# Cross-attention on one core: first Wq chunk in three transfers, second x block on two queues, and a new written order

## The chip, the cores and the metric

The kernel runs on one core of one Trainium2 chip. The metric is the device time of one execution in microseconds; smaller is better. The times shown are medians over runs of the same program.

## The reference, cut to what matters

The input x has 2 batches of 2048 tokens with 640 channels; the context has 2 batches of 154 tokens with 1024 channels, the first 77 of them text, the other 77 of a second kind ("ip"). There are 20 heads of 32 channels. All is fp32.

```python
q = split_heads(x @ Wq.T, 20)
k, v       = split_heads(text @ Wk.T),    split_heads(text @ Wv.T)
k_ip, v_ip = split_heads(ip @ Wk_ip.T),   split_heads(ip @ Wv_ip.T)
attend = lambda q, k, v: softmax(q @ k.T / sqrt(32)) @ v
out = merge_heads(attend(q, k, v)) + merge_heads(attend(q, k_ip, v_ip))
return out @ Wo.T + bo + x
```

## The kernel before, in words

The matrices reach the kernel transposed, so that the contracted dimension lies on the 128 partitions. The 640 channels are 5 chunks of 128, four heads to a chunk. The tokens of a batch are four blocks of 512, two to a half-batch. A **unit** u is one chunk of one half-batch: u = 0 to 19, in pairs; the pair 2q, 2q+1 is the attention number q (chunk q mod 5 of batch q div 5).

The work of a unit, by the words of the written order:

- `q.u.h`: five 128x512 matmuls on PE (TensorE, L195) make the queries of block h; `cq.u.h` copies and scales them on ACT (ScalarE, L205).
- `R0.u`, `R1.u`, `R2.u`: scores of the unit's three groups of token tiles (L233), each into four PSUM banks. A group has 3 tiles (24 PE records a group, since an fp32 product counts twice), in odd units 3, 2 and 2. The ninth tile of an even unit's third group belongs to the next unit, so `R2.0` needs `cq.1.0` for its last tile.
- `K` copies the four banks to SBUF on ACT (L245), `M` takes row maxima on DVE (VectorE, L258), `S` subtracts them (L272; on POOL, the GpSimd engine, or with the suffix `.d` on DVE), `E` is the exponential on ACT (L279), `D` and `I` sum and invert on DVE (L304, L311), `N` multiplies (L316, POOL), `T` transposes on DVE (L323).
- `A.q`: attention (L332) for both units of q, after all six `T`; `CA.q` copies the result on ACT.

Around it stand the key and value products `k.c.t`, `v.c.t` (L134, eight 128x154 matmuls, 16 PE records, one for each chunk c and kind t of context) with their copies `ck`, `cv`, and a detour of the values: `SQ` transposes them on DVE (L144), `VW` writes them to DRAM, `VS` reads them back spread over partitions. The output projection of batch 0 uses seven products in place of eight on sums of blocks (`W`, `G` on POOL or DVE at L404 and L434, products `m` at L493 and L503, `o` at L474, sums `cm`, `co`), that of batch 1 another scheme of 33 products (`F` at L857, weight and token sums `V` at L835 and L837 and `X` at L843, output sums `Y` at L803 and L805). Loads are words too: `LK` a key or value weight, `LQ` a Wq chunk, `LX` a block of x of batch 1.

Every engine works its instructions strictly in the order in which they are written, and that order is one long list of words, `SCHEDULE`, worked off by `emit`. The word after `@` names the PSUM banks, `.d` or `.p` the engine of a sum. The list sets what PE meets when, and which of DVE and POOL does a subtraction or a small sum. In front of it the opening is written out by hand:

```python
queues = nc.sync, nc.scalar
for k in range(NC):
    load_x(queues[k % 2])
    queues[1 - k % 2].dma_start(out=wqs[0][:, k, :], in_=WqT[ts(k, P), :P])
for _ in range(NC):
    load_x()
```

A transfer is issued by SP (SyncE, `nc.sync`) or by ACT (`nc.scalar`). Eight semaphores serve them in turn, so the issue of each transfer waits until the one eight places before it has landed; what stands behind it on its queue waits too. Names in the orders below: bank_79 to bank_86 are the banks 0 to 7, x_92 to x_95 the four blocks of x, wq_87 and wq_88 the two places for Wq chunks, aT the place of the key and value weights.

Of the kernel before, what the change touches and what calls it, by code (L numbers as in the profile page):

```python
# [9 lines left out]
F32 = mybir.dt.float32  # L10
# [10 lines left out]
def kernel(  # L21
# [25 lines left out]
    nc = tc.nc  # L47
# [5 lines left out]
    NH = 2  # L53
# [471 lines left out]
    slices.extend((i, k) for i in range(NHB) for k in range(NC))  # L525
    queues = nc.sync, nc.scalar
    for k in range(NC):
        load_x(queues[k % 2])
        queues[1 - k % 2].dma_start(out=wqs[0][:, k, :], in_=WqT[ts(k, P), :P])
    for _ in range(NC):  # L530
        load_x()
    load_wq(1)
    half = NCC // 2
    for k in (0, half):
        nc.sync.dma_start(  # L535
            out=wo_ct[:, ds(k * B * LT, half * B * LT)].rearrange("p (k n) -> p k n", k=half),
            in_=ctxT[ds(k * P, half * P), :].rearrange("(k p) n -> p k n", p=P),
        )
        load_w(k // half)
    for _ in range(NH * NC):  # L540
        load_x()
    load_w(2)
    load_w(3)
    nc.sync.dma_start(out=bo_sb, in_=bo.rearrange("(c p) -> p c", p=P))
# [5 lines left out]
    FIRST = ((0, 0), (0, 1), (2, 0))  # L550
    for n, (u, h) in enumerate(FIRST):
        queries(u, h, banks[G + n])
        take_queries(u, h, banks[G + n])
    for t in range(2):

        ps = halves[t][G - 2 + t]
        project_kv(t, ps)
        for b in range(B):
            nc.scalar.copy(kT[:, 0, b, t, :], keys_in(ps)[:, b])  # L559
# [82 lines left out]
    def emit(word):  # L642
# [27 lines left out]
        elif k == "fe":  # L670
            fetch(x, PARTS[y])
        elif k == "LO":
            load_wo()
        elif k == "LF":
            for part in PARTS:
                fetch(0, part)
# [223 lines left out]
```

## Time and profile before

| | |
|---|---|
| median of 3 runs | 498.87 us (498.44 to 499.19) |
| profiled execution | 499.62 us |
| its span, first to last instruction | 497.8 us |
| TensorE clock granted | 1.00 |
| PE, DVE, POOL, ACT busy | 98%, 89%, 80%, 49% of the span |
| moved by DMA | 70.15 MB, mean 141 GB/s |

How its lines are read. In the timeline a row is: start in us, length, engine, line, operation, output tile <- input tiles, shapes, count; in brackets the idle time just before it and what ended that. PEld is the weight load of PE, SPq and ACTq are the DMA issues of SP and ACT. A wait row is: engine and line that waited <- engine or transfer waited for, us in total, times, longest. A row of the chain (the work that ended last, followed back) is: start, length, engine, tile, line, count. A group row is: line, engine, operation, names, shapes, count | busy us, mean ns | idle us before and its releasers. A row by stretches of time is: from:to, length, then the busy us of PE, PEld, DVE, ACT and POOL, the granted clock, the DMA share and GB/s.

### The profile page before, as it was taken

Reading aid. Unit: us, or ns where it says so; the run is one execution under the profiler, and the core shown is the slowest. Engines: PE = TensorE matmul, PEld = TensorE weight load, DVE = VectorE, ACT = ScalarE, POOL = GpSimd, SP = SyncE. Lnnn points to the kernel's source line nnn. Section 1 sums busy time; section 2 is a strip of 40 time slices with the busy share of each in tenths; the row PEclk is TensorE's granted clock in tenths of the full one; section 3 lists DMA queues with packets and bytes.
Section 4 is the critical chain, followed back from the end, with each engine's and each line's share of the span. In section 5 each row is a group of like instructions: output and inputs, shape, how many; then the busy total and the mean of one; then the engine's idle time right before and its main releaser. Section 6 shows DMA issues by size and latency. Waiting matters only on the chain.

```text
span 497.8 us, 9753 instructions
## 1 busy us (share of the span) xinstructions
PE 489.1 (98%) x4114; PEld 287.1 (58%) x4114; DVE 440.8 (89%) x407; ACT 241.7 (49%) x423; POOL 398.4 (80%) x170
## 2 busy tenths in 40 slices
PE   8999999999999999999999999999999999999997
PEld 4658545667449555556656677565555565444442
DVE  0078999999997999999995999999999999997995
ACT  1157666667646677658526734325687561100000
POOL 0009997999959999999967799996998999349691
PEclk9999999999999999999999999999999999999999
DMA  8972640241915628826047525671375012410026
GB/s 276 353 201 68 163 112 1 66 103 49 260 42 183 178 77 269 310 80 224 18 144 260 170 84 162 213 255 47 121 255 182 18 35 77 156 67 19 0 95 243
DMA packets 66988, 70.15 MB, mean 141 GB/s; under 512 B 3712, under 2 KB 46720, under 8 KB 66944
## 3 DMA queue, kind: packets, MB, share of 16 engines
q1 hardware_dynamic: 66224, 68.81, 43.8%
q8 instruction: 32, 0.52, 0.4%
q10 hardware_dynamic: 720, 0.72, 0.4%
q14 instruction: 12, 0.10, 0.1%
HBM read 58.21 MB, written 11.30 MB: 140 GB/s over the span
## 4 chain that ended last, share of the span: by engine, by line
PE 88%; DMA 4%; DVE 4%; SPq 2%; ACT 1%; issue 1%; ACTq 0%
PE bank L195 32%; PE bank L857 11%; PE bank L332 11%; PE bank L233 10%; PE bank L493 9%; PE bank L134 8%; PE bank L474 4%; PE bank L503 2%; DMA x<-in_x_dram 2%; DVE pb L323 2%; DMA aT<-in_L_xattn_Wv_dram 2%; SPq L167 1%; DVE den L304 1%; SPq L535 1%; SPq L124 0%
## 5 line engine op out<-in xcount | busy, mean ns | idle before, releaser
L272 POOL TENSOR_TENSOR pb<-pb,mx 128x1848 f32<-128x1848 f32 (+1 forms) x54 | 160.2, 2980 | 52.8 <-DVE mx L258 52.7
L316 POOL TENSOR_TENSOR pb<-pb,rden 128x1848 f32<-128x1848 f32 (+1 forms) x59 | 172.2, 2935 | 14.8 <-ACT aT L355 5.9
L195 PE MATMUL bank<-x,wq 128*128 128x512 f32 x400 | 179.9, 599 | 0.9 <-DMA x<-in_x_dram 0.8
L258 DVE TENSOR_REDUCE mx<-pb 128x24 f32<-128x1848 f32 (+1 forms) x60 | 109.4, 1842 | 34.6 <-ACT pb L245 34.5
L195 PEld LDWEIGHTS bank<-x,wq 128*128 128x128 f32 x400 | 73.7, 190 | 85.9 <-issue 81.0
L245 ACT COPY pb<-bank 128x462 f32<-128x462 f32 (+1 forms) x240 | 102.2, 533 | 40.3 <-PE bank L233 37.9
L279 ACT ACTIVATE pb<-pb 128x1848 f32<-128x1848 f32 (+1 forms) x60 | 94.3, 1590 | 51.3 <-POOL pb L272 49.5
L323 DVE STREAM_TRANSPOSE pb<-pb 128x1920 f32<-128x1920 f32 (+1 forms) x60 | 114.1, 1922 | 2.1 <-POOL pb L316 1.8
L304 DVE TENSOR_REDUCE den<-pb 128x24 f32<-128x1848 f32 (+1 forms) x60 | 109.8, 1836 | 1.2 <-ACT pb L279 0.8
L233 PEld LDWEIGHTS bank<-kT,qT 32*128 32x128 f32 x1280 | 44.8, 184 | 24.9 <-issue 17.9
L233 PE MATMUL bank<-kT,qT 32*128 32x154 f32 x1280 | 55.9, 305 | 0.6 <-ACT kT L559 0.3
L332 PE MATMUL bank<-pb,v 32*32 32x512 f32 x1600 | 55.3, 597 | 0.7 <-DVE pb L323 0.6
L134 PEld LDWEIGHTS bank<-wo_ct,aT 128*128 128x128 f32 x320 | 43.2, 188 | 7.3 <-issue 3.5
L134 PE MATMUL bank<-wo_ct,aT 128*128 128x154 f32 x320 | 45.7, 296 | 1.4 <-DMA aT<-in_L_xattn_Wv_dram 1.0
L205 ACT ACTIVATE qT<-bank 128x512 f32<-128x512 f32 x40 | 23.9, 602 | 46.1 <-PE bank L195 46.1
L332 PEld LDWEIGHTS bank<-pb,v 32*32 32x32 f32 x1600 | 29.5, 103 | 23.0 <-issue 11.3
L474 PE MATMUL bank<-aT,wo_ct 128*128 128x512 f32 x80 | 36.3, 595 | 0.0
L493 PE MATMUL bank<-aT,wo_ct 128*128 128x256 f32 x128 | 32.8, 389 | 0.1
L493 PEld LDWEIGHTS bank<-aT,wo_ct 128*128 128x128 f32 x128 | 23.3, 190 | 7.0 <-issue 3.9
L805 DVE TENSOR_TENSOR x<-x,bank 128x512 f32<-128x512 f32 x36 | 23.3, 682 | 3.6 <-PE bank L857 3.5
L474 PEld LDWEIGHTS bank<-aT,wo_ct 128*128 128x128 f32 x80 | 15.0, 190 | 16.4 <-issue 15.6
L857 PE MATMUL bank<-pb 128*128 128x512 f32 x48 | 22.7, 594 | 0.0
(74 smaller groups left out, 351.1 us busy)
## 6 DMA issues: line engine op xcount, KB each, us to landing
x<-in_x_dram SPq DMA_DIRECT2D x20, 1280.0 KB, 7.2
out_dram<-acc SPq DMA_DIRECT2D x20, 256.0 KB, 2.5
x<-in_x_dram SPq DMA_DIRECT2D x18, 256.0 KB, 5.4
acc<-in_x_dram SPq DMA_DIRECT2D x16, 256.0 KB, 3.9
out_dram<-x SPq DMA_DIRECT2D x15, 256.0 KB, 2.1
v<-scr SPq DMA_DIRECT2D x40, 80.0 KB, 3.5
wq<-in_L_xattn_Wq_dram SPq DMA_DIRECT2D x9, 320.0 KB, 4.5
aT<-in_L_xattn_Wk_dram SPq DMA_DIRECT2D x5, 512.0 KB, 5.5
```

The source lines that it names most:

```text
L134: nc.tensor.matmul(keys_in(out), loaded[n][:, k, :], cT[:, k, :, t, :], start=(k == 0), stop=(k == NCC - 1))
L195: nc.tensor.matmul(pq, wqs[q % 2][:, k, :], xs[place_of(u, h)][:, k, :], start=(k == 0), stop=(k == NC - 1),)
L233: nc.tensor.matmul(ps[g][:, ts(t, 2 * L)], qTs[(v, h)][g * D : (g + 1) * D, ts(st, P)], kT[g * D : (g + 1) * D, c, b].rearrange("p t l -> ...
L245: nc.scalar.copy(keys_of(u, s)[:, :, g], ps[g][:, : n * 2 * L].rearrange("p (n l) -> p n l", n=n))
L258: nc.vector.tensor_reduce(mx, rows_of(u, s), AX.X, ALU.max, negate=by_rows(u, s))
L272: eng.tensor_tensor(rows_of(u, s), rows_of(u, s), maxs[(u, s)].unsqueeze(3).to_broadcast([P, n, 2, L]), ALU.subtract)
L279: nc.scalar.activation(e, e, AF.Exp)
L304: nc.vector.tensor_reduce(dens[(u, s)], rows_of(u, s), AX.X, ALU.add)
L316: eng.tensor_tensor(rows_of(u, s), rows_of(u, s), rdens[(u, s)].unsqueeze(3).to_broadcast([P, n, 2, L]), ALU.mult)
L323: nc.vector.transpose(p, p)
L332: nc.tensor.matmul(pa[r][g * D : (g + 1) * D, :], v4[rows, g, k, :], zones[rows, :, g, k, :], start=(k == 0), stop=(k == NK - 1),)
L493: nc.tensor.matmul(part, w_of[m][:, kp, op], t_of(m, b, i)[:, kp], start=(op == kp == 0 and m in (1, 2, 5)), stop=(op == 1 and kp == 1 and ...
```

## The change

Three edits.

1. The first Wq chunk goes in three transfers (128, 256 and 256 rows) in place of five, and the five slices of the second x block alternate between ACT's and SP's queue in place of SP alone.
2. What stood written out between these loads and the list (the loads of the second Wq chunk, the context, the first four key and value weights, the third and fourth x block and the bias; the first three query products; the first two key products) becomes words at the head of the list: `LQ.1 LC.0 LK.0 ...`. PE's order up to the second key product is the same as before; the copies of the first keys stay two for each product.
3. The list is another one. Its words are the same beside the new head; their order, the banks, and the engine of some sums differ. Up to `A.9`, the subtractions S1.0, S0.10, S1.15, S1.17 and the sums G5.0, G4.0, G5.1 go from DVE to POOL, and S0.1, S1.10, S1.13 from POOL to DVE. Behind it 22 of the `V` sums stood on DVE before and 15 do now; of the `X` sums ten did and ten do, not all the same.

The diff, with the list cut to its first lines:

```diff
-    slices.extend((i, k) for i in range(NHB) for k in range(NC))
+    slices.extend((i, k) for i in range(NH) for k in range(NC))
     queues = nc.sync, nc.scalar
+    WQ_PARTS = (0, 1), (1, 3), (3, NC)
     for k in range(NC):
         load_x(queues[k % 2])
-        queues[1 - k % 2].dma_start(out=wqs[0][:, k, :], in_=WqT[ts(k, P), :P])
-    for _ in range(NC):
-        load_x()
-    load_wq(1)
-    half = NCC // 2
-    for k in (0, half):
+        if k < len(WQ_PARTS):
+            ks = slice(*WQ_PARTS[k])
+            queues[1 - k % 2].dma_start(
+                out=wqs[0][:, ks, :],
+                in_=WqT[ks.start * P : ks.stop * P, :P].rearrange("(k p) o -> p k o", p=P),
+            )
+    for k in range(NC):
+        load_x(queues[1 - k % 2])
+
+    def load_context(n):
+        half = NCC // 2
...
-        load_w(k // half)
-    for _ in range(NH * NC):
-        load_x()
-    load_w(2)
-    load_w(3)
-    nc.sync.dma_start(out=bo_sb, in_=bo.rearrange("(c p) -> p c", p=P))
...
-    FIRST = ((0, 0), (0, 1), (2, 0))
-    for n, (u, h) in enumerate(FIRST):
-        queries(u, h, banks[G + n])
-        take_queries(u, h, banks[G + n])
-    for t in range(2):
-
-        ps = halves[t][G - 2 + t]
-        project_kv(t, ps)
-        for b in range(B):
-            nc.scalar.copy(kT[:, 0, b, t, :], keys_in(ps)[:, b])
...
-        "R0.0@5476 LK.5 K0.0 M0.0 S0.0.d R1.0@2103 K1.0 M1.0 S1.0.d q.1.0@5 cq.1.0 v.0.0@3 cv.0.0 R2.0@5047 K2.0 "
...
+        "LQ.1 LC.0 LK.0 LC.1 LK.1 lx.2.0 lx.2.1 lx.2.2 lx.2.3 lx.2.4 lx.3.0 lx.3.1 lx.3.2 lx.3.3 lx.3.4 LK.2 LK.3 LB q.0.0@4 cq.0.0 q.0.1@5 cq.0.1 q.2.0@6 cq.2.0 k.0.0@2 ck.0.0 k.0.1@7 ck.0.1 "
+        "R0.0@6754 K0.0 R1.0@1320 K1.0 q.1.0@6 cq.1.0 M0.0 S0.0.d R2.0@5407 M1.0 S1.0 K2.0 M2.0 S2.0 R0.1@2316 "
...
+        elif k == "LC":
+            load_context(x)
+        elif k == "LB":
+            nc.sync.dma_start(out=bo_sb, in_=bo.rearrange("(c p) -> p c", p=P))
+        elif k == "lx":
+            nc.sync.dma_start(out=xs[x][:, y], in_=xT[ts(y, P), ts(x, TB)])
```

More of the change, by code (lines that the diff above doesn't have):

```diff
@@ L522, in take_product @@
             nc.vector.tensor_tensor(t, t, ps.rearrange("p (op t) -> p op t", op=2), ALU.add)
-    slices.extend((i, k) for i in range(NHB) for k in range(NC))
+    slices.extend((i, k) for i in range(NH) for k in range(NC))
     queues = nc.sync, nc.scalar
+    WQ_PARTS = (0, 1), (1, 3), (3, NC)
     for k in range(NC):
         load_x(queues[k % 2])
-        queues[1 - k % 2].dma_start(out=wqs[0][:, k, :], in_=WqT[ts(k, P), :P])
-    for _ in range(NC):
-        load_x()
-    load_wq(1)
-    half = NCC // 2
-    for k in (0, half):
+        if k < len(WQ_PARTS):
[8 more added lines that the diff above has]
+        half = NCC // 2
         nc.sync.dma_start(
-            out=wo_ct[:, ds(k * B * LT, half * B * LT)].rearrange("p (k n) -> p k n", k=half),
-            in_=ctxT[ds(k * P, half * P), :].rearrange("(k p) n -> p k n", p=P),
-        )
-        load_w(k // half)
-    for _ in range(NH * NC):
-        load_x()
-    load_w(2)
-    load_w(3)
-    nc.sync.dma_start(out=bo_sb, in_=bo.rearrange("(c p) -> p c", p=P))
+            out=wo_ct[:, ds(n * half * B * LT, half * B * LT)].rearrange("p (k n) -> p k n", k=half),
+            in_=ctxT[ds(n * half * P, half * P), :].rearrange("(k p) n -> p k n", p=P),
+        )
     warm = pb[:, 0].rearrange("p g l -> p (g l)")[:, :P]
@@ L696, in emit @@
         elif k == "ck":
-            nc.scalar.copy(kT[:, x, :, y, :], keys_in(at[name[1:]]))
+            if x:
+                nc.scalar.copy(kT[:, x, :, y, :], keys_in(at[name[1:]]))
+            else:
+                for n in range(B):
+                    nc.scalar.copy(kT[:, x, n, y, :], keys_in(at[name[1:]])[:, n])
         elif k == "cv":
```

136 rows, old and new, of the table SCHEDULE are left out of this document.

## The prediction

> **What bounds the kernel now.** I read the page's busy times first, then the waits of PE, the chain that ended last, the opening in order of time, and the idle time of DVE and POOL.
>
> ```profile
> PE 489.1 (98%) x4114; PEld 287.1 (58%) x4114; DVE 440.8 (89%) x407; ACT 241.7 (49%) x423; POOL 398.4 (80%) x170
> ```
>
> PE (TensorE) works 489.1 of 497.8 us. Neither order adds or drops a matmul, so what can change is PE's idle time and the cost of passing from one kind of matmul to another. The waits of PE (total, times, longest, in us):
>
> ```profile
> PE bank L134 <- DMA aT<-in_L_xattn_Wv_dram: 1.0, 1, 1.0
> PE bank L195 <- DMA x<-in_x_dram: 0.8, 1, 0.8
> PE bank L332 <- DVE pb L323: 0.6, 1, 0.6
> PE bank L134 <- ACT pb L245: 0.5, 1, 0.5
> PE bank L857 <- ACT aT L360: 0.3, 1, 0.3
> PE bank L233 <- ACT kT L559: 0.3, 1, 0.3
> PE bank L233 <- ACT pb L245: 0.3, 1, 0.3
> ```
>
> Beside the start of the program these seven rows are all its idle time: 3.8 us, and that is about the whole prize. But PE is not alone. The waits of DVE and POOL:
>
> ```profile
> DVE mx L258 <- ACT pb L245: 34.5, 11, 25.3
> POOL pb L272 <- DVE mx L258: 52.7, 12, 36.7
> ```
>
> DVE's longest wait is the opening (25.3 us); after it DVE waits for copies only 9 us in all until the last attention. It is nearly as full as PE, and attention A.q can't start before the last transpose T of its two half-batches. How close that is, at A.1 and A.9 (timeline and chain, transpose first, then PE):
>
> ```profile
> 110.64 1.51 DVE L323 STREAM_TRANSPOSE pb<-pb 128x1280 f32<-128x1280 f32 x1 [0.52 <-POOL pb L316]
> 112.44 5.45 PE bank L332 x150
> 426.19 1.50 DVE L323 STREAM_TRANSPOSE pb<-pb 128x1280 f32<-128x1280 f32 x1
> 427.74 5.52 PE L332 MATMUL bank<-pb,v 32*32 32x512 f32 x160 [0.61 <-DVE pb L323]
> ```
>
> T2.3 ends at 112.15 and A.1 follows 0.3 us later; T2.19 ends at 427.69 and A.9 follows at once, having waited 0.6. So PE's time is worth something only where DVE keeps up.
>
> **The opening.** The same bytes in the same order of need, but 8 transfers instead of 10 for the first block and its weights. Each transfer waits at issue for the one eight places before it. Timeline and DMA rate (last column GB/s):
>
> ```profile
> 4.13 4.21 SPq L167 DMA_DIRECT2D x<-in_x_dram  x6
> 4.32 0.34 ACTq L529 DMA_DIRECT2D wq<-in_L_xattn_Wq_dram  x1
> 4.35 2.90 PE L195 MATMUL bank<-x,wq 128*128 128x512 f32 x6
> 8.04 10.57 PE L195 MATMUL bank<-x,wq 128*128 128x512 f32 x24 [0.80 <-DMA x<-in_x_dram]
> 3.50:4.00 0.50, 0.50 (x5) 0.50 (x3) 0.00 (x0) 0.00 (x0) 0.00 (x0) 1.00 1.06 388
> 6.50:7.00 0.50, 0.50 (x2) 0.00 (x0) 0.00 (x0) 0.00 (x0) 0.00 (x0) 1.00 1.00 208
> 7.00:7.50 0.50, 0.24 (x1) 0.00 (x0) 0.00 (x0) 0.00 (x0) 0.00 (x0) 1.00 0.69 240
> 10.06 0.60 ACT L205 ACTIVATE qT<-bank 128x512 f32<-128x512 f32 x1 [4.09 <-PE bank L195]
> ```
>
> The ninth and tenth (last x slice, last Wq part) go out only at 4.13 and 4.32, and two us later the rate dips. What SP issues at the start, before and after (x_92 is the first block of x, x_93 the second, wq_87 and wq_88 the Wq chunks):
>
> ```order
> L167 DMA x_92<-in_x_dram 128x512
> L529 DMA wq_87<-in_L_xattn_Wq_dram 128x128
> L167 DMA x_92<-in_x_dram 128x512
> L529 DMA wq_87<-in_L_xattn_Wq_dram 128x128
> L167 DMA x_92<-in_x_dram 128x512 [waits DMAHW1_49]
> L167 DMA x_93<-in_x_dram 128x512 [waits DMAHW2_49]
> ```
>
> ```order
> L167 DMA x_92<-in_x_dram 128x512
> L532 DMA wq_87<-in_L_xattn_Wq_dram 128x2x128
> L167 DMA x_92<-in_x_dram 128x512 x2
> L167 DMA x_93<-in_x_dram 128x512 [waits DMAHW1_49]
> L167 DMA x_93<-in_x_dram 128x512 [waits DMAHW3_49]
> L186 DMA wq_88<-in_L_xattn_Wq_dram 128x5x128 [waits DMAHW5_49]
> ```
>
> Everything the first five products need now goes without a wait, and wq_88 follows two x_93 slices instead of five; ACT issues the other three, ahead of its table load. Against 388 GB/s the two slow rows lack (180 + 148) x 0.5 = 164 KB, 0.4 us of stream. PE's six passes took 8.04-4.35 = 3.69 us for 6 x 0.43 = 2.58 (0.43 is 4.29 us over ten, below): 1.1 lost. The price lies between 0 (if the dip only moves) and -1.1; I take **-0.7**, between the stream's 0.4 and PE's 1.1: PE soon needs the Wk_ip that comes later in the same stream.
>
> The Trainium skill (DMA: Bandwidth & Descriptors, section Issuing engines are not separate DMA queues) says that transfers begun on several engines share the same 16 DMA engines and that only issue time is saved. By it this term would be 0 if the stream were full throughout; the 208 GB/s row says it was not.
>
> **The Wv wait.** PE, from the second use of wq_87 (q.1.0) on, before and after; L134 is a key or value product, L233 scores:
>
> ```order
> L233 MATMUL bank_82<-kT,qT_1_159 128x154
> L195 MATMUL bank_84<-x_94,wq_87 128x512 x5
> L134 MATMUL bank_82<-wo_ct,aT 128x154 x8
> L233 MATMUL bank_84<-kT,qT_1_159 128x154
> L233 MATMUL bank_79<-kT,qT_1_159 128x154
> ```
>
> ```order
> L233 MATMUL bank_79<-kT,qT_1_157 128x154
> L195 MATMUL bank_85<-x_94,wq_87 128x512 x5
> L233 MATMUL bank_84<-kT,qT_1_157 128x154
> L233 MATMUL bank_83<-kT,qT_1_157 128x154
> L233 MATMUL bank_79<-kT,qT_1_157 128x154
> ```
>
> The value product v.0.0 moved behind R2.0, R0.1 and q.1.1. Chain and ACT:
>
> ```profile
> 22.64 7.96 DMA aT<-in_L_xattn_Wv_dram
> 25.21 4.56 PE L195 MATMUL bank<-x,wq 128*128 128x512 f32 x10
> 29.81 0.60 ACT L205 ACTIVATE qT<-bank 128x512 f32<-128x512 f32 x1 [1.72 <-PE bank L195]
> 36.01 4.06 DVE L258 TENSOR_REDUCE mx<-pb 128x24 f32<-128x1848 f32 x2 [1.32 <-ACT pb L245]
> ```
>
> Wv lands at 30.60 and PE will ask for it at 25.2 (where q.1.0 began) - 0.7 + 2 x 4.49 + 2 x 1.00 (a product and a run of scores, rows of the next part) = 35.5: **-1.0**. Late next: the third tile of R2.0 needs the copy of q.1.0 (0.60 us), and two tiles, 0.5 us, cover most of it: 0 to 0.6, I take **+0.2**. DVE's 1.32 us wait ahead of M2.0, which stood behind the same Wv, goes too.
>
> **Runs of scores.** From the chain:
>
> ```profile
> 339.54 4.49 PE bank L195 x10
> 349.52 1.00 PE bank L233 x24
> 240.28 4.29 PE bank L195 x10
> 171.98 1.78 PE bank L233 x48
> ```
>
> 24 more scores cost 0.78 us, so a run has a fixed 1.00-0.78 = 0.22, and the product after it takes 4.49 for 4.29: 0.42 us a run. Counted along PE, the old order has 47 runs, the new 46: **-0.4**.
>
> **Before A.1.** DVE ahead of T2.3, before and after:
>
> ```order
> L258 TENSOR_REDUCE mx_0_760<-pb 128x24
> L323 STREAM_TRANSPOSE pb<-pb 128x1920
> L323 STREAM_TRANSPOSE pb<-pb 128x1280
> L258 TENSOR_REDUCE mx_2_822<-pb 128x24
> L323 STREAM_TRANSPOSE pb<-pb 128x1280
> ```
>
> ```order
> L144 STREAM_TRANSPOSE wo_ct<-vT 128x160 x2
> L258 TENSOR_REDUCE mx_2_837<-pb 128x24
> L311 RECIPROCAL rden_2_839<-den_2_756 128x16
> L323 STREAM_TRANSPOSE pb<-pb 128x1920
> L258 TENSOR_REDUCE mx_1_844<-pb 128x24
> L323 STREAM_TRANSPOSE pb<-pb 128x1280 x2
> ```
>
> Two pieces more stand ahead of it: the maxima mx_1_844 and the pair of vT transposes (S1.0 leaving DVE and S0.1 coming cancel). Their rows, with those of the next part:
>
> ```profile
> L258 DVE TENSOR_REDUCE mx<-pb 128x24 f32<-128x1848 f32 x40 | 81.5, 2055 | 29.4 <-ACT pb L245 29.3
> L144 DVE STREAM_TRANSPOSE wo_ct<-vT 128x160 f32<-128x160 f32 x10 | 2.6, 303 | 0.0
> L272 DVE TENSOR_TENSOR pb<-pb,mx 128x1232 f32<-128x1232 f32 x2 | 2.9, 1456 | 0.1
> L434 DVE TENSOR_TENSOR x<-aT 128x512 f32<-128x512 f32 x2 | 2.3, 1130 | 0.0
> L434 DVE TENSOR_TENSOR aT<-aT 128x512 f32<-128x512 f32 x1 | 0.7, 651 | 0.0
> L272 POOL TENSOR_TENSOR pb<-pb,mx 128x1232 f32<-128x1232 f32 x18 | 40.3, 2249 | 4.1 <-DVE mx L258 4.1
> L434 POOL TENSOR_TENSOR aT<-aT 128x512 f32<-128x512 f32 x7 | 10.8, 1545 | 0.0
> 59.05 2.11 PE bank L134 x16
> 30.51 2.07 DVE L258 TENSOR_REDUCE mx<-pb 128x24 f32<-128x1848 f32 x1
> ```
>
> 2.06 + 0.61 = 2.7 us. T2.3 comes at 112.15 + 2.7 - 0.7 (opening) - 1.3 (Wv) = 112.8. PE has one key product more ahead of A.1 (2.11) and comes at 112.4 + 2.1 - 1.9 (the terms so far) = 112.6. That is a wait of 0.2; if the 1.3 us of DVE come back at another place and the new order has none of PE's old waits on ACT on the way, it is 2.0; if DVE idles less, 0. I take **+0.5**, near the worked value, with a little for the new order's own DVE waits.
>
> **Before A.9.** DVE gives POOL four subtractions and takes three (net one of the short kind, 1.46), and gives up three L434 sums (2 x 1.13 + 0.65): 4.4 us. The last transpose can so end at 427.7 - 4.4 - 0.7 = 422.6, and PE comes at 427.1 - 1.4 = 425.7: **-0.6**. POOL takes them at 2.25 + 3 x 1.55 = 6.9 us. What hides this is an earlier start: its first subtraction is now S1.0, after M1.0 (30.51 + 2.07 - 0.7 = 31.9), where it was S2.0, after M2.0 (36.01 + 2.03 = 38.0); and 16 us of the L272 row's idle lie outside the start. If that cover fails, POOL is late for the last transposes and the 0.6 stays.
>
> PE's four waits on ACT (1.4 us) belong to places of the old order; the new one keeps banks about as tight, so I set old against new at 0 (from -0.8 to +0.8). After A.9 the last products and sums keep their engines' load, but 7 small sums go from DVE to POOL, which idles there: 0.
>
> **Sum:** -0.7 - 1.0 + 0.2 - 0.4 + 0.5 - 0.6 = -2.0. The profiled execution took 499.62 (span 497.8 and 1.8 around it) and becomes 497.6. It lay 0.75 above the median of 498.87, which becomes **496.9**.
>
> **Rivals.** About 0.2%, 1.0 us, is what a measurement here can tell from nothing.
> 1. *The opening stays* (the page's rule, and DMA share at 0.69 in one row only): -1.3, 497.6. Chance 0.08.
> 2. *DVE and POOL are full:* A.1 waits its 2.0 and A.9 keeps its wait: -0.7 - 1.0 + 0.2 - 0.4 + 2.0 = +0.1, 499.0. For it: T2.3 and T2.19 both ended within 0.3 us of attention. Against: 4.4 us less DVE work. Chance 0.18.
> 3. *Slower: ACT's queue.* An exponential waits for POOL's subtraction with copies behind it on ACT:
>
> ```profile
> 69.87 1.75 ACT L279 ACTIVATE pb<-pb 128x1848 f32<-128x1848 f32 x1 [4.02 <-POOL pb L272]
> ```
>
> Before this the wait was covered. If one of 4.0 us falls between A.0 and A.1, DVE's maxima stop, T2.3 slips by as much, and A.1 waits 4.5: -2.0 + 4.0 = +2.0, 500.9. It decides once A.1 waits over 3.5 us. Against: S1.0 reaches POOL while it is empty. Chance 0.19.
>
> Forecast: 0.55. Faster 0.55 + 0.08 = 0.63, same 0.18, slower 0.19. The range takes the good ends (-1.1 in the opening, no wait at R2.0 or A.1, 0.8 of the ACT waits gone: -1.1 - 1.0 - 0.4 - 0.6 - 0.8 = -3.9, 495.0) and rival 3 up to its own time, 500.9, with half of its chance above. The forecast's own range is 495.0 to 497.8.
>
> **What would show it.** Right: the first query copy on ACT near 9.3 instead of 10.06; no Wv row among PE's waits; A.1 waiting under 1.5 us; A.9 without a DVE wait. Wrong: the rate dip still there; an L332 wait above 3.5 us; ACT idle before L279 with PE waiting for L245.

## The result, and the profile after

The changed kernel takes 505.06 us, median of 4 runs (504.49 to 505.33), beside 499.03 for the kernel before (4 runs, 498.44 to 499.21): 1.0121 times as long, 95% interval 1.0104 to 1.0139. It is slower, by 6.0 us, where 496.9 and "faster" were forecast and the range ended at 500.9. The profiled execution of the changed kernel took 504.49 us, span 502.4, against 499.62 and 497.8 before.

The waits of PE after, beside the start of the program:

```profile
PE bank L858 <- DVE x L806: 2.6, 1, 2.6
PE bank L134 <- issue: 0.6, 1, 0.6
PE bank L134 <- ACT pb L245: 0.5, 1, 0.5
PE bank L493 <- issue: 0.4, 1, 0.4
PE bank L858 <- ACT aT L360: 0.3, 1, 0.3
PE bank L233 <- ACT kT L698: 0.3, 1, 0.3
PE bank L332 <- issue: 0.2, 1, 0.2
```

Without the first row they are 2.3 us, 1.5 less than before. The first row is new, and it lies behind A.9, in the stretch that the prediction had dismissed in one sentence.

A.9 starts at 427.74 before and at 427.93 after (first row below): up to there these two executions show nothing won and 0.2 us lost. From there to the end of the span it is 497.8 - 427.7 = 70.1 us before and 502.4 - 427.9 = 74.5 after. So the tail has 4.4 of the 4.6 us between the two spans. The two executions lie 0.6 us above their median (before) and 0.6 below it (after), so they show less than the 6.0 us between the medians; where the rest lies, the experiments tell. DVE and POOL there, one instruction to a row, the two engines mixed in order of time:

```profile
427.93 5.52 PE L332 MATMUL bank<-pb,v 32*32 32x512 f32 x160
445.49 2.35 POOL L844 TENSOR_TENSOR pb<-aT 128x1024 f32<-128x1024 f32 x1
445.51 3.40 DVE L844 TENSOR_TENSOR pb<-aT 128x1024 f32<-128x1024 f32 x1
447.79 3.32 POOL L844 TENSOR_TENSOR pb<-aT 128x1024 f32<-128x1024 f32 x1
448.84 3.36 DVE L844 TENSOR_TENSOR x<-aT 128x1024 f32<-128x1024 f32 x1
451.08 1.43 POOL L838 TENSOR_TENSOR pb<-wo_ct,pb 128x128 f32<-128x128 f32 x1
452.12 1.27 DVE L806 TENSOR_TENSOR x<-x,bank 128x512 f32<-128x512 f32 x2
452.94 4.51 PE L858 MATMUL bank<-aT,pb 128*128 128x512 f32 x6 [2.58 <-DVE x L806]
```

Read the ends: POOL's first sum (X.V) ends at 447.84; DVE's X.G, started beside it, ends 1.08 later, at 448.91; POOL's X.F ends 2.20 after that, at 451.11; DVE's X.B 1.09 later, at 452.20. One at a time, each with about its own length, in turn. How long these sums take by themselves shows in the same line's lengths of DVE in the kernel before (L843; ns, least, median and most) and after (L844):

```profile
L843 DVE TENSOR_TENSOR pb<-aT x5: 1216/1218/1226, 433.3 to 461.3; 128x1024 f32<-128x1024 f32 x5
L844 DVE TENSOR_TENSOR pb<-aT x4: 1211/1476/3402, 433.5 to 445.5; 128x1024 f32<-128x1024 f32 x4
L844 DVE TENSOR_TENSOR x<-aT x4: 1220/1620/3360, 428.8 to 468.2; 128x1024 f32<-128x1024 f32 x4
```

Behind X.B on DVE stand the two additions (452.12) that empty the banks for F29. So PE pauses for 2.58 us, and then it is slow as well. The same place by stretches of 1 us (PE's busy time, its granted clock; the two rows left out have 0.50 too):

```profile
453.00:454.00 1.00, 1.00 (x3) 0.93 0.00 0
454.00:455.00 1.00, 1.00 (x3) 0.50 0.00 0
...
457.00:458.00 1.00, 1.00 (x3) 0.86 0.00 0
```

For 0.14 + 3 + 0.28 = 3.4 us the clock stands at half, and matmuls start 0.85 us apart instead of 0.43. The pause of 2.75 us (from start to start, less the usual 0.43) and 1.7 us for the slow clock (half of 3.4) make 4.45, as much as the tail lost; what each is worth by itself, the experiments below ask.

**Theory 1**, to be tested: DVE and POOL take turns when both add two tiles of the SBUF, the new tail puts two long pairs of such sums just ahead of F29, and PE's pause makes the clock fall. **Rival 2**: the tail has too much work left for DVE and POOL, whatever its order. **Rival 3**: the cause lies ahead of A.9 and shows only behind it. The Trainium skill (SBUF — State Buffer, section SBUF: two separate sides, Who interferes with whom) has theory 1 as a rule: a DVE instruction with two SBUF inputs contends with a GpSimd instruction that reads the SBUF, not with one that only writes it. The rows above agree with its first half (1.22 us alone, 3.40 in turns).

### The profile page after: what moved, and what is told of

It is laid out like the page before. It is cut to its first block, busy times and chain, and to the rows that moved or that the text cites. A ratio compares the mean times of both kernels' runs of the same rounds, so it can differ in the third digit from the quotient of the medians.

```text
span 502.4 us, 9755 instructions
## 1 busy us (share of the span) xinstructions
PE 492.1 (98%) x4114; PEld 288.5 (57%) x4114; DVE 444.6 (88%) x396; ACT 241.6 (48%) x423; POOL 414.2 (82%) x181
## 3 DMA queue, kind: packets, MB, share of 16 engines
q10 hardware_dynamic: 1136, 1.51, 0.9%
## 4 chain that ended last, share of the span: by engine, by line
PE 82%; DVE 12%; issue 2%; ACT 2%; DMA 1%; POOL 1%
PE bank L195 32%; PE bank L858 10%; PE bank L233 9%; PE bank L134 9%; PE bank L332 9%; PE bank L493 8%; DVE den L304 3%; PE bank L474 3%; DVE pb L323 3%; DVE mx L258 2%; PE bank L503 2%; DMA wq<-in_L_xattn_Wq_dram 1%; DVE pb L844 1%; ACT pb L245 1%; DVE acc L518 0%
## 5 line engine op out<-in xcount | busy, mean ns | idle before, releaser
L332 PEld LDWEIGHTS bank<-pb,v 32*32 32x32 f32 x1600 | 29.6, 103 | 22.8 <-issue 13.5
```

The source lines that it names most:

```text
L332: nc.tensor.matmul(pa[r][g * D : (g + 1) * D, :], v4[rows, g, k, :], zones[rows, :, g, k, :], start=(k == 0), stop=(k == NK - 1),)
```

## The experiments

All times are medians; "before" beside them was 498.9 to 499.1.

**Heads and tails exchanged.** The list was cut behind A.9 and the halves were crossed.

```diff
 # e1
 ... A.9@1032          # the changed kernel's list up to here
+V.D.0.p V.P.0.d X.A.d@1 X.L.d@3 CA.9 F31.1@0 ...   # the tail of before
 # e2
 ... A.9@0             # the list of before up to here
+V.E.0.p CA.9 V.G.0.d V.U.0.d V.U.1.d st.3.4 ...    # the new tail
```

> The changed kernel's order up to and with A.9, then the order that the kernel before has behind A.9 (V.D.0 and V.P.0, which the changed kernel does later, stand at its head; sums and stores that are already done are left out of it). Theory 1 (DVE and POOL take turns when both add two tiles from the SBUF, and in the new tail two long sums on each fall together just ahead of F29): the tail takes about 70.1 us again instead of 74.5, so 505.1 - 4.4 = 500.7. Rival 2 (the tail is late because the new order up to A.9 leaves more sums to it, whatever their order): at least 504. Rival 3 (the loss lies ahead of A.9 and only shows behind it): 505.

> The mirror image: the order of the kernel before up to and with A.9, then the changed kernel's order behind A.9 (V.E.0 and four stores that it has done by then are put in). Theory 1: 499.0 + 4.4 = 503.4, with the same two long DVE sums of some 3.4 us. Rivals 2 and 3: 499 to 500.

Measured: 500.49 for the new head with the old tail (1.0035 of before, 1.0022 to 1.0048), 504.06 for the old head with the new tail (1.0105, 1.0090 to 1.0120). The loss of the tail goes with its order: rival 2 falls, and rival 3 falls for the larger part. For a smaller part it holds: the new head with the old tail is still 1.4 us slower than the 499.11 beside it, with an interval wholly above 1, where the prediction had the head 2.0 us faster. DVE's long sums in the first are all short again, and in the second, where the additions start behind X.G and X.B as in the changed kernel, they are long:

```profile
L841 DVE TENSOR_TENSOR pb<-aT x5: 1215/1217/1224, 433.8 to 461.6; 128x1024 f32<-128x1024 f32 x5
```

```profile
428.04 6.56 PE L332 MATMUL bank<-pb,v 32*32 32x512 f32 x138 [1.86 <-DVE pb L323]
447.88 1.64 DVE L840 TENSOR_TENSOR pb<-aT 128x1024 f32<-128x1024 f32 x1
449.45 3.36 DVE L840 TENSOR_TENSOR x<-aT 128x1024 f32<-128x1024 f32 x1
453.56 2.95 PE L854 MATMUL bank<-aT,pb 128*128 128x512 f32 x6 [0.88 <-DVE x L802]
```

In the second the pause ahead of F29 is only 0.88 us and the clock holds there. It fell earlier, at A.9, after a pause of 1.86 us (by stretches; the granted clock is the third number from the end, PEclk):

```profile
429.00:430.00 1.00, 1.00 (x36) 0.56 (x32) 1.00 (x2) 0.00 (x0) 0.00 (x0) 0.61 0.91 348
430.00:431.00 1.00, 1.00 (x34) 0.48 (x4) 1.00 (x6) 0.00 (x0) 0.00 (x0) 0.50 0.10 37
```

So this execution has another split than the changed kernel's. Nor does the clock fall in every execution: its mean was 1.00 in two of the five of this kernel, where 3.4 us at half speed would leave 0.997.

**One sum later, on DVE.**

```diff
-X.G.d@10 F24.0 F1.0 X.B.d@0 V.O.1.p F20.1 Y6.1.11 Y6.0.11 F7.0@4
+F24.0 F1.0 X.B.d@0 V.O.1.p F20.1 Y6.1.11 Y6.0.11 X.G.d@10 F7.0@4
```

> The changed kernel with one word moved: X.G.d on DVE stands behind Y6.1.11 and Y6.0.11 instead of ahead of X.B.d. Theory 1: X.B.d still waits for POOL's first long sum (3.4 us), but the two additions that F29 waits for come 3.4 us earlier, PE's pause of 2.6 us goes, and the clock stays at 1.00: 505.1 - 4.4 = 500.7, or 501.5 if X.G.d makes a later sum late. Theory 1 without the clock (the pause alone costs): 502.4. Rival 2: 504 or more, since the amount of work is the same.

Measured: 502.83 (1.0074, 1.0061 to 1.0088), half of what was expected.

```profile
446.83 3.40 DVE L841 TENSOR_TENSOR x<-aT 128x1024 f32<-128x1024 f32 x1
451.34 2.18 DVE L841 TENSOR_TENSOR pb<-aT 128x1024 f32<-128x1024 f32 x1
454.89 1.12 PE L855 MATMUL bank<-aT,pb 128*128 128x512 f32 x2 [1.51 <-DVE acc L801]
```

X.B (446.83) still waits for POOL, as expected, F29 no longer waits; but X.G, now behind the first additions, waits for POOL's other sum (2.18) with the next additions behind it. A pause of 1.51 us came back there; this one left the clock at 1.00. The wait had moved by one place.

**The same sum on POOL.**

```diff
-X.G.d@10
 ... X.F.p@11
+X.G.p@10
```

> The changed kernel with one sum moved: X.G goes from DVE to POOL, right behind X.F. Theory 1: DVE has only X.B left beside POOL's two long sums and takes turns with one of them, its additions ahead of F29 come 3.4 us earlier, and unlike in the run with X.G later on DVE nothing is put between them and the next additions: PE has no pause, clock 1.00, 505.1 - 4.4 = 500.7. If POOL's later sums become late instead: 502 to 503.

Measured: 500.58 (1.0036, 1.0023 to 1.0050), as expected of theory 1.

```profile
445.15 3.43 DVE L841 TENSOR_TENSOR x<-aT 128x1024 f32<-128x1024 f32 x1
445.15 7.97 POOL L841 TENSOR_TENSOR pb<-aT 128x1024 f32<-128x1024 f32 x3
448.51 1.27 DVE L803 TENSOR_TENSOR x<-x,bank 128x512 f32<-128x512 f32 x2
```

One word moved to the slower engine (2.36 us a sum instead of 1.22) makes the kernel 4.5 us faster. POOL's three sums take 7.97 us, 0.9 more than three times their own length, for the one DVE sum between them; the additions start at 448.51, 3.6 us earlier than in the changed kernel, and PE has no wait ahead of F29.

**What it takes to collide.** Three kernels leave the order alone and change the form of the instructions beside each other.

```diff
 # e4: X.V and X.F on POOL
-nc.gpsimd.tensor_tensor(places[w], ra, rb, op)
+nc.gpsimd.memset(places[w], 0.0)
 # e5: X.V and X.F on POOL
+nc.gpsimd.tensor_scalar(places[w], ra, -1.0, None, ALU.mult)
 # e6: X.G and X.B on DVE
+nc.vector.tensor_scalar(places[w], ra, -1.0, None, ALU.mult)
```

> The changed kernel, with X.V and X.F on POOL written as fills with zero that read nothing (these two sums are left out). Theory 1: DVE's X.G and X.B beside them take 1.2 us each instead of 3.4, PE's pause ahead of F29 goes, 500.7. If POOL's writes are what DVE waits for: DVE's two sums stay long by as much as POOL's fills last. If DVE's sums are long for a reason of their own (their operands' places): 3.4 us each and 505.

> The changed kernel, with X.V and X.F on POOL written as products of one tile with -1 (their second input is left out). If what collides is any POOL instruction that reads the SBUF against a DVE sum of two SBUF tiles: X.G and X.B take about 3.4 us each again, 505. If it needs two inputs on both engines: 1.2 us each, 500.5. A sentence of the Trainium skill (SBUF — State Buffer, There are two physically separate sides) counts a DVE instruction with two SBUF inputs as colliding with any GpSimd one that reads the SBUF: by that rule 505.

> The changed kernel, with X.G and X.B on DVE written as products of one tile with -1 (their second input is left out), POOL as in the changed kernel. If the turns need two SBUF inputs on DVE: at most 1.2 us each beside POOL's sums, no pause ahead of F29, 500.5. If a DVE instruction with one SBUF input collides as well: each still waits for a POOL sum of 2.36 us, so some 3 us each and 503 to 505. The Trainium skill (SBUF — State Buffer, There are two physically separate sides) lets a DVE instruction collide also when it uses both ports for one input: by that rule the second case.

Measured: 500.46 with POOL filling (1.0026, 1.0017 to 1.0036), 500.78 with POOL reading one tile, 503.30 with DVE reading one (one run each for the last two). Rows of the three, POOL and DVE beside each other:

```profile
446.19 1.84 POOL L842 MEMSET pb<- 128x1024 f32 x2
446.22 1.22 DVE L844 TENSOR_TENSOR pb<-aT 128x1024 f32<-128x1024 f32 x1
447.36 1.22 DVE L844 TENSOR_TENSOR x<-aT 128x1024 f32<-128x1024 f32 x1
```

```profile
445.27 5.89 POOL L842 TENSOR_SCALAR pb<-aT 128x1024 f32<-128x1024 f32 x2
445.29 2.10 DVE L844 TENSOR_TENSOR pb<-aT 128x1024 f32<-128x1024 f32 x1
447.31 1.21 DVE L844 TENSOR_TENSOR x<-aT 128x1024 f32<-128x1024 f32 x1
```

```profile
445.89 5.10 POOL L844 TENSOR_TENSOR pb<-aT 128x1024 f32<-128x1024 f32 x2
445.92 2.87 DVE L842 TENSOR_SCALAR pb<-aT 128x1024 f32<-128x1024 f32 x1
448.71 2.83 DVE L842 TENSOR_SCALAR x<-aT 128x1024 f32<-128x1024 f32 x1
```

POOL that only writes does not hold DVE up at all, and the whole 4.5 us come back: it is not the writing that collides. A DVE instruction of one SBUF input and a constant takes turns with POOL's sums too (2.87 us, ending 0.55 after POOL's). The Trainium skill (SBUF — State Buffer, Who interferes with whom) names both cases, the second as the mode in which DVE uses both its ports for one input, and these two runs agree with it. The middle run agrees less: by the rule any POOL instruction that reads should block, but X.B ran in its normal 1.21 us beside POOL's one-input form and X.G in 2.10. What that form takes by itself no run here shows, so this stays open.

**The clock.** More products of F4.0's form were put into PE's pause and summed into F4.0's bank.

```diff
-F29.1 F29.0
+F4.0 F4.0 F4.0 F4.0 F4.0 F4.0 F29.1 F29.0     # e7
+F4.0 F4.0 F4.0 F29.1 F29.0                    # e10
```

> The changed kernel with six more matmuls of F4.0's form ahead of F29.1, 6 x 0.43 = 2.58 us, in the pause of 2.58 us (they are summed into F4.0's bank, so the two sums out of that chain are not those of the reference). Theory 1 with the clock as a second step (the pause of PE makes the clock fall to half for 3.4 us, 1.7 us lost): PE no longer pauses, the granted clock stays 1.00, and the time falls by 1.7 to 503.4. If the clock fell for another reason: no change, 505.1. If the added matmuls reach beyond the pause: up to 505.5.

> The changed kernel with three more products of F4.0's form ahead of F29.1. A product is two matmuls of 0.43 us, so six matmuls or 2.58 us, as long as PE's pause (the sums out of F4.0's chain are not those of the reference). If the pause makes the clock fall: no fall, the pause's time stays, 505.1 - 1.7 = 503.4. If the clock falls for another reason: 505.1.

The first of the two was miscounted: a product is two matmuls, so six are 5.15 us, 2.4 more than the pause. It took 505.55 (1.0136, 1.0121 to 1.0150), clock 1.00: 2.4 us of work more and only 0.5 us slower, so by estimate 1.9 saved; X.C takes its usual 1.22 us there and no later start of PE slips. The second fits the pause: 504.15 (1.0106, 1.0092 to 1.0120), clock 1.00 throughout.

```profile
448.38 4.46 PE L856 MATMUL bank<-pb,wo_ct 128*128 128x512 f32 x10
452.86 2.95 PE L856 MATMUL bank<-aT,pb 128*128 128x512 f32 x6
456.52 2.57 DVE L842 TENSOR_TENSOR x<-aT 128x1024 f32<-128x1024 f32 x1
461.15 1.10 PE L856 MATMUL bank<-aT,pb 128*128 128x512 f32 x2 [0.19 <-DVE acc L802]
```

With the pause filled the clock stayed at 1.00 in all eight executions of the two kernels, and without it it fell in three of the changed kernel's four: the fall goes with the pause. What it costs is less clear. Filling the pause gave back 0.9 us in the medians, not 1.7, and the two intervals overlap (1.0092 to 1.0120 here, 1.0104 to 1.0139 for the changed kernel). In the traces it is 0.3: the stretch from A.9 to the end takes 502.0 - 427.8 = 74.2 us here and 74.5 in the changed kernel. And the one execution of the changed kernel with a mean clock of 1.00 was its longest, 505.33 us. One reason can be read off the rows: F29 now runs at full speed, and PE then meets waits that the slow stretch had covered, X.C's collision (2.57 us) among them; its starts slip four times, by 0.2, 0.35, 0.4 and 0.2 us. So the slow clock costs about 1.7 us where it falls, but in this order removing it gains 0.9 at most; at least 3.5 of the 4.4 us of the tail belong to the turns.

**The opening, and a sum of the kernel before.** In before, V.P.0 on DVE stands ahead of T2.19, for which A.9 waits, and takes 1.08 us where such a sum takes 0.28; two POOL instructions lie beside it:

```profile
423.46 2.24 POOL L316 TENSOR_TENSOR pb<-pb,rden 128x1232 f32<-128x1232 f32 x1
425.19 1.08 DVE L837 TENSOR_TENSOR pb<-wo_ct 128x128 f32<-128x128 f32 x1
425.67 0.45 POOL L837 TENSOR_TENSOR pb<-wo_ct 128x128 f32<-128x128 f32 x1
```

It ends at 426.27, just behind the second. Three kernels apply this and the new opening to the kernel before.

```diff
 # e8 and e11: the new opening (WQ_PARTS, second block's x on two queues)
 # e11 and e12
-V.D.0.p V.P.0.d T2.19 A.9@0
+V.D.0.p T2.19 V.P.0.d A.9@0
```

> The kernel before with the new opening alone: first Wq chunk in three transfers, the second block's x slices on two queues, its own order of instructions behind that. What the prediction gave it: opening -0.7, the wait for Wv -1.0 (Wk_ip landed 1.2 us earlier in the changed kernel), so 497.3 against 499.0. What the traces of the first runs suggest: the fourth x slice landed at 7.9 to 8.1 with the new opening as in the profiled run before, so the opening itself 0, and only the wait for Wv goes, where a run has it: 498.0 to 499.0.

> The kernel before with the new opening, and with V.P.0 on DVE behind T2.19 instead of ahead of it. In the profiled run before, V.P.0 took 1.08 us at 425.19 instead of 0.28, until POOL's N2.19 was done, and T2.19, which A.9 waits for, started 0.5 us later for it. Theory 1 (turns): A.9 starts 0.5 us earlier, 498.6 - 0.5 = 498.1, and both kernels are beaten. If V.P.0's length had another reason: 498.3 to 498.6.

> The kernel before with V.P.0 alone behind T2.19, the old opening. Theory 1 (turns): 499.0 - 0.5 = 498.5. If the opening is worth what the run with the opening alone showed (0.3), 0.3 slower than the run with both.

Measured: the opening alone 498.58 (0.9990, 0.9981 to 0.9999), the sum alone 498.51 (0.9990, 0.9981 to 0.9999), both 498.45 (0.9989, 0.9980 to 0.9997). Each is faster than before, by 0.3 to 0.6 us against the median beside it, with intervals that end just below 1; that the two add up can't be seen at this size. The kernel with both missed the 498.1 of theory 1 and lies where the other reading had it (498.3 to 498.6), so its time does not tell the two apart. Its rows speak for theory 1: A.9's wait fell from 0.61 to 0.19, and V.P.0 behind T2.19 is as short as any:

```profile
425.78 0.25 DVE L840 TENSOR_TENSOR pb<-wo_ct 128x128 f32<-128x128 f32 x1
425.91 5.52 PE L332 MATMUL bank<-pb,v 32*32 32x512 f32 x160 [0.19 <-DVE pb L323]
```

## Why the prediction was wrong

**The step that failed most** is the last one before the sum: "After A.9 the last products and sums keep their engines' load, but 7 small sums go from DVE to POOL, which idles there: 0". The number of long sums on each engine was indeed kept; what changed is which sums of the two engines lie beside each other. The term measures +4.4 us in the traces (70.1 to 74.5) and +4.5 in the runs (505.06 to 500.58 for one word). It had no bound above zero and no rival of its own: rival 3, the one on the slower side, put the loss in ACT's queue between A.0 and A.1, which the trace does not show. The term is 4.5 of the 8.2 us between 496.9 and 505.06. No row of DVE or POOL behind A.9 was read, though 70 us of the kernel lie there and PE waited 0.3 us in all of it, so that any sum that came late had to show.

**What could have been read beforehand.** The group rows of before gave DVE's long sums as one length, 1216 to 1226 ns: in that order none of them lay beside a long POOL sum. But V.P.0's 1.08 us was in the trace, four times its usual length, and with it the rule that a change of order has to be checked against.

**The opening: -0.7 predicted, about 0 measured.** The first query copy came at 10.20, not near 9.3, and the first scores start at 23.32 before and 23.28 after. Fourteen traces, three with the old opening and eleven with the new, show what was misread:

| | old (3) | new (11) |
|---|---|---|
| last transfer of the first x block and its weights landed | 7.56, 7.56, 8.39 | 7.68 to 8.49, median 8.05 |
| first query copy on ACT | 8.87, 9.69, 10.06 | 9.81 to 10.62, median 10.22 |
| Wk_ip landed | 20.59, 20.59, 20.81 | 19.20 to 20.00 |
| first scores on PE | 23.32, 23.33, 23.54 | 22.88 to 23.70, median 23.29 |
| Wv landed | 29.24, 29.38, 30.60 | 27.95 to 29.40 |

The profiled run before was the one with the latest landing of the three (8.39). The dip in its rate, from which the prediction worked out its price, was that execution's; the new opening does not land the first block earlier at all. What it does do is land Wk_ip 1 us earlier. Neither moves the first scores, since each opening is held up at another place; PE's rows with the old opening (first, of the kernel with the sum alone) and with the new one (of the new head with the old tail):

```profile
4.20 13.97 PE L195 MATMUL bank<-x,wq 128*128 128x512 f32 x30
20.64 2.38 PE L134 MATMUL bank<-wo_ct,aT 128*128 128x154 f32 x16 [0.36 <-DMA aT<-in_L_xattn_Wk_ip_dram]
```

```profile
8.22 10.54 PE L195 MATMUL bank<-x,wq 128*128 128x512 f32 x24 [0.86 <-DMA x<-in_x_dram]
18.60 4.38 PE L134 MATMUL bank<-wo_ct,aT 128*128 128x154 f32 x32
```

The old one makes PE wait for Wk_ip, the new one for x. (The changed kernel's own profile has no wait for x: its first matmuls start 1.01, 0.85 and 0.59 us apart, so that x is there in time. 0.85 is the spacing that the half clock gave at F29; in the packed trace the record of the full clock begins at 6.72 us here and at 4.00 before.) The rival "the opening stays" was right on this term: in runs the new opening alone took 498.58 beside 498.90, 0.3 us with its effect on the Wv wait in it.

**The Wv wait: -1.0 predicted, -1.0 in these two traces, less in general.** The row is gone after. But of the three traces with the old order and the old opening ahead of it, only the profiled run before had the wait: Wv landed there at 30.60, in the others at 29.24 and 29.38, in time for PE at 29.6; with the new opening and the old order it was 0.2. That execution lay 0.75 above the median, and a part of the two largest gains was in this excess; the sum took them off the span and the excess off once more.

**A.1 and A.9.** A.9's term was right: its wait for DVE is gone (-0.6 predicted). A.1 has no row among the waits, where +0.5 was set, and the copy of q.1.0 cost nothing (+0.2). The one run of scores less (-0.4) can't be told apart in the traces. PE's waits on ACT went from 1.4 us to 1.1, near the 0 that was set.

**The second step that failed: the sum of these terms, -2.0 up to A.9, where the runs show +1.4.** The new head with the old tail took 500.49 beside 499.11, and the changed kernel with the one sum moved 500.58 beside 499.03. So some 1.5 of the 6.0 us were lost ahead of A.9. The execution that the prediction started from hides it, because the Wv wait made it late. In the nine traces with the new head A.9 starts at 427.57 to 429.82, median 428.18 (first row, the new head with the old tail); the old order behind the new opening, with a Wv wait of 0.2 only, has it at 426.58 (second row):

```profile
428.18 5.52 PE L332 MATMUL bank<-pb,v 32*32 32x512 f32 x160
426.58 5.52 PE L332 MATMUL bank<-pb,v 32*32 32x512 f32 x160 [0.63 <-DVE pb L323]
```

The prediction had nothing on its list that could make the new order slower there without a wait on another engine. What came are the waits that the profile puts to nothing but "issue", 1.2 us in three rows of the changed kernel. Such rows stand in all nine traces with the new head, between 0.8 and 2.6 us in all, and in none of the five with the old order. They are about as large as the loss. Their cause was not tried and stays open.

## What to carry to other kernels

When a reordering leaves every engine's load as it was, compare which instructions of DVE and POOL lie side by side: an elementwise sum of two SBUF tiles on DVE waits out a whole POOL sum, and what stands behind it on DVE waits too. A sum whose length in the trace is a multiple of its usual one is the sign; move it to the other engine, or behind what PE waits for, and look where the collision goes. A gain read off one profiled execution's waits on DMA needs a second execution before it is priced. And where two orders differ in several stretches, cross them: the runs of head and tail exchanged priced each half, where the two traces showed one loss only.

## What the runs showed of the hardware

- DVE and POOL took turns to within 0.2 us: 2.35 and 1.22 us sums lying beside each other ended one after the other, with 3.40 and 3.32 us from start to end. POOL fills beside DVE sums did not hold DVE up (1.22 us each).
- In the profiled executions the clock fell after PE pauses of 1.86 and 2.58 us, not after 1.51, and stayed at half for 3.4 us both times (0.39 and 0.32 of a us in the rows at its ends at A.9 of the crossed kernel, doubled, and 2 us between). The fall came 1.2 and 0.9 us after PE had started again, and in other executions of the same two kernels (one of four, two of five) the mean clock stayed at 1.00. The Trainium skill (TensorE: Matmul & The Clock Gate, Part 1: The HAM clock gate (the "warmup" mystery)) puts the fall behind an idle window of about 3.4 us and the return behind a busy one as long; the half-speed time agrees with that length, the pauses that sufficed are shorter, and the measurement decides.
